# Batch 0's distances as float32r parts, the last product in two sets of columns, and a new order of loads

## The chip, the cores and the metric

The kernel runs on one core of one Trainium2 chip. A core has five engines that run their own instruction streams: TensorE (PE in the profile; its weight loads are PEld), VectorE (DVE), ScalarE (ACT), GpSimd (POOL) and SyncE (SP), which here issues all DMAs. The metric is the device time of one execution in microseconds (us). Before the change it is 393.94 us, the median of three runs (393.58 to 394.14).

## The reference

The inputs are x (4 batches, 256 tokens, 512 features), a context `ctx` (4, 64, 512), a table `fside` (4, 256, 256), a mask and weights, all float32. Four layers follow each other:

- L0, a mixture of low-rank updates: router weights `w = softmax(x @ router_W.T + b)`, `a_sum[b,s,r] = sum over a of x[b,s] . ctx[a,r]`, and `x = nan_to_num(x + 0.5 * sum_n w_n * (a_sum @ lora_B[n].T))`.
- L1, cross attention of 256 tokens on 64 context rows with 32 heads, an output product, a residual sum and a layer norm.
- L2 and L3, the same function twice, each with four blocks. Its core is:

```python
sq = jnp.sum(xyz * xyz, axis=1)                     # xyz = ctx: 64 coordinates, 512 points
d2 = sq[:, :, None] + sq[:, None, :] - 2.0 * jnp.einsum('bdn,bdm->bnm', xyz, xyz)
_, idx = jax.lax.top_k(-d2, 8)                      # 8 nearest points, once per batch
# in each block i:
c  = jnp.einsum('oi,bin->bon', w_center[i], p)      # p = leaky_relu(points)
gn = jnp.einsum('oi,bikn->bokn', w_neighbor[i], g)  # g = p gathered at idx
points = (c + gn.sum(axis=2)) / 9.0 + shortcut
```

`w_center` and `w_neighbor` are both `fside`, so a block is one product of `p` with `fside[i]` and one product with a 512 x 512 matrix of zeros and ones, "own point plus eight nearest".

## The kernel before

**A planner writes the order.** The functions of the kernel do not issue instructions. They add operations to a `Plan` (lines 63 to 167): engine, assumed cost, the tiles it reads and writes. `emit` then simulates all engines with those costs and always emits the operation that can start first; among operations of one engine that can start within 0.05 us the lowest `rank` wins. The rank is a due time: the entry of `DEADLINES` for the operation's batch (line 33) less the longest tail of work behind it. PSUM banks (8), SBUF buffers by kind, and the DVE/POOL shared port are resources of the simulation. The result is a fixed order per engine; on the chip each engine runs its order strictly, with semaphore waits. So any edit to an operation, a cost, a due time or the list of loads can move instructions everywhere.

**Loads.** `load` (line 258) adds DMAs on SP, in the order of the calls in lines 287 to 311, later ones through `load_xT` and `load_x` in the loop over batches. There are eight DMA semaphores, used in turn, so the ninth load waits for the first.

**Start.** PE runs 20 products of 128 columns on a constant (line 320) while the first loads travel. `keys` (line 677) makes K transposed from `WkT` and `ctxT` in four groups `kT`; `mixture` (line 386) makes the router logits and the low-rank input `route`; DVE turns them into `z`; `mix` (line 490) transposes `z` on PE (`zT`), multiplies by `lora_BT` (`upd`, line 505), adds to `x` (line 520), handles NaN and infinities (`hi`, `lo`, `odd`, copy_predicated in line 530) and transposes to `x1T`. `values` (line 731) makes V (`v`, then `vbd` on DVE, line 755), `queries` (line 764) Q (`q`, line 775), `attention` (line 798) the rest of L1.

**Distances.** `nearest` (line 614) takes four banks `d2_b_j` of 128 x 512, each holding x.x' - |x'|^2 / 2 for 128 points against all 512. For each bank DVE finds the eight largest (`top`, line 622) and replaces them (`rest`, line 625), ACT makes zeros and ones (`near`), POOL adds the identity, an SP DMA transposes, ACT stores `nbr`. For batches 1 to 3 `scores` (line 579) splits x into a float32r part and its exact rest, stacked on 128 partitions as `chl` and `clh`, and uses three float32r products a bank (lines 603 to 605); the rests are made on POOL. For batch 0 `scores_first` (line 544) uses float32 products with K = 64, two banks side by side in the upper and lower half of the array, which is why `ctx[0]` is loaded twice, into both halves of `cxx0`; only the squares are split (line 574).

**Blocks.** `block` (line 955) is done 8 times for each batch: ACT makes `p` (line 961), PE `wp` in float32 (line 972), ACT and DVE split it into `wph` and `wpl` (lines 985 and 988), PE multiplies both with `nbr` in float32r (line 1003, four products for each half of the points and each half `o` of the output), and DVE adds to `x` (line 1015). After the last block a DMA stores each 128 x 512 half (line 1025).

## Time and profile before

| | |
|---|---|
| median of 3 runs | 393.94 us |
| the profiled execution's own time | 394.15 us |
| its span, first to last instruction | 392.1 us |
| PE busy | 381.6 us (97%), 2116 products |
| PEld busy | 292.4 us (75%) |
| DVE busy | 226.8 us (58%) |
| ACT busy | 217.0 us (55%) |
| POOL busy | 105.3 us (27%) |
| mean granted TensorE clock | 0.996 |

Products are pipelined, so "busy" counts a product from its start to its modelled end and two neighbours overlap; the distance between two starts, the pitch, tells what a product costs in a stream. The chain of waits is followed back from the last instruction. A window gives the busy time of each engine between two times, the granted TensorE clock (1.00 is full speed) and what the DMAs moved.

### The profile page before, as it was taken

How to read it: one execution, taken by the hardware profiler on the slowest of the kernel's cores; microseconds unless marked ns; L12 is line 12 of the kernel's file. 1: busy time of each engine (PE TensorE's matmuls, PEld its weight loads, DVE VectorE, ACT ScalarE, POOL GpSimd, SP SyncE). 2: the span in 40 equal slices, each digit the busy share in tenths (PEclk: the TensorE clock that was granted, in tenths of full speed). 3: DMA queues.
4: the chain of work that ended last, by engine and by line, in shares of the span. 5: the costliest groups of instructions: out<-in, count | busy, mean ns of one | idle time of the engine just before them, and what ended most of it. 6: DMA issues, size and time to landing. Idle time of an engine off the chain costs nothing.

```text
span 392.1 us, 5547 instructions
## 1 busy us (share of the span) xinstructions
PE 381.6 (97%) x2116; PEld 292.4 (75%) x2116; DVE 226.8 (58%) x412; ACT 217.0 (55%) x335; POOL 105.3 (27%) x116
## 2 busy tenths in 40 slices
PE   8998999999999999999999999999999999999996
PEld 5847846657776866878767766888888888888884
DVE  2479799997796656945982524632433334324333
ACT  2651763966795989995697962333333422333330
POOL 4896204848205605640034220500000000000000
PEclk9998999999999999999999999999999999999999
DMA  6999320152401552434005411000000001000002
GB/s 185 369 381 354 69 54 0 28 109 44 91 15 24 115 80 54 63 72 82 1 2 99 90 28 55 0 0 2 0 0 2 0 0 55 0 1 2 0 0 107
DMA packets 47241, 25.80 MB, mean 66 GB/s; under 512 B 43184, under 2 KB 43312, under 8 KB 46576
## 3 DMA queue, kind: packets, MB, share of 16 engines
q1 hardware_dynamic: 47216, 25.46, 26.2%
q8 instruction: 16, 0.26, 0.3%
q14 instruction: 9, 0.07, 0.1%
HBM read 12.87 MB, written 2.10 MB: 38 GB/s over the span
## 4 chain that ended last, share of the span: by engine, by line
PE 71%; DVE 15%; ACT 8%; DMA 3%; issue 2%; SPq 1%; DVEq 0%; ACTq 0%
PE blk L1003 29%; PE wp L972 25%; PE q L775 4%; PE o L922 4%; PE upd L505 3%; PE kT L683 2%; DVE rest L625 2%; DMA WkT<-in_WkT 1%; DVE den L857 1%; PE avT L902 1%; DVE mx L842 1%; DVE s L848 1%; DVE top L622 1%; DMA pT_t<-pT_a 1%; ACT pTs L482 1%
## 5 line engine op out<-in xcount | busy, mean ns | idle before, releaser
L972 PE MATMUL wp<-fT,p 128*128 128x256 f32 x512 | 119.7, 380 | 1.4 <-ACT p L961 1.4
L1003 PE MATMUL blk<-nbr,wph 128*128 128x512 f32 x256 | 112.4, 439 | 0.3 <-ACT wph L985 0.3
L972 PEld LDWEIGHTS wp<-fT,p 128*128 128x128 f32 x512 | 96.3, 189 | 18.6 <-ACT p L961 2.4
L1003 PE MATMUL blk<-nbr,wpl 128*128 128x512 f32 x256 | 100.6, 393 | 0.7 <-DVE wpl L988 0.7
L1015 DVE SCALAR_TENSOR_TENSOR x<-blk,x 128x512 f32<-128x512 f32 x64 | 43.6, 686 | 72.3 <-PE blk L1003 72.2
L985 ACT CAST wph<-wp 128x512 fp32r<-128x512 f32 x64 | 37.2, 586 | 79.1 <-PE wp L972 79.0
L988 DVE TENSOR_TENSOR wpl<-wp,wph 128x512 fp32r<-128x512 f32 x64 | 43.7, 686 | 47.5 <-ACT wph L985 47.5
L961 ACT ACTIVATE p<-x 128x512 f32<-128x512 f32 x64 | 39.9, 629 | 35.2 <-DVE x L1015 34.1
L1003 PEld LDWEIGHTS blk<-nbr,wph 128*128 128x128 f32 x256 | 48.2, 188 | 13.0 <-issue 1.8
L1003 PEld LDWEIGHTS blk<-nbr,wpl 128*128 128x128 f32 x256 | 48.2, 188 | 12.7 <-DVE wpl L988 1.8
L879 POOL TENSOR_TENSOR s<-s,rden 128x512 f32<-128x512 f32 x32 | 32.3, 1043 | 70.5 <-DVE rden L869 41.4
L922 PE MATMUL o<-WoT,avTs 128*128 128x512 f32 x64 | 30.0, 598 | 0.3 <-ACT avTs L916 0.2
L775 PE MATMUL q<-x1T,WqT 128*128 128x256 f32 x128 | 29.2, 380 | 0.7 <-ACT x1T L457 0.7
L505 PE MATMUL upd<-lora_BT,zTs 128*128 128x512 f32 x64 | 28.7, 596 | 0.0
L482 ACT COPY pTs<-pT_t 128x1024 uint16<-128x1024 uint16 x24 | 27.1, 1160 | 1.4 <-DMA pT_t<-pT_a 1.2
L775 PEld LDWEIGHTS q<-x1T,WqT 128*128 128x128 f32 x128 | 24.2, 190 | 4.4 <-ACT x1T L457 1.0
L463 ACT COPY pT_a<-s 128x1024 uint16<-128x1024 uint16 x24 | 24.5, 1043 | 1.0 <-DMA pT_t<-pT_a 0.8
L854 ACT ACTIVATE s<-s 128x512 f32<-128x512 f32 x32 | 18.8, 625 | 9.1 <-DVE s L848 9.1
L842 DVE TENSOR_REDUCE mx<-s 128x8 f32<-128x512 f32 x32 | 20.1, 678 | 4.1 <-PE s L816 4.1
L505 PEld LDWEIGHTS upd<-lora_BT,zTs 128*128 128x128 f32 x64 | 11.9, 190 | 13.1 <-issue 12.2
L857 DVE TENSOR_REDUCE den<-s 128x8 f32<-128x512 f32 x32 | 20.1, 674 | 1.8 <-ACT s L854 1.7
L947 POOL TENSOR_TENSOR x<-x,rows 128x512 f32<-128x512 f32 x8 | 10.4, 1305 | 37.1 <-DVE x L942 37.1
(112 smaller groups left out, 402.2 us busy)
## 6 DMA issues: line engine op xcount, KB each, us to landing
xT<-in_xT SPq DMA_DIRECT2D x4, 512.0 KB, 7.5
x<-in_x SPq DMA_DIRECT2D x4, 512.0 KB, 11.8
out<-x SPq DMA_DIRECT2D x8, 256.0 KB, 2.0
WkT<-in_WkT SPq DMA_DIRECT2D x4, 256.0 KB, 7.4
lora_BT<-in_lora_BT SPq DMA_DIRECT2D x1, 1024.0 KB, 9.2
WvT<-in_WvT SPq DMA_DIRECT2D x1, 1024.0 KB, 10.4
rows<-in_rows SPq DMA_DIRECT2D x2, 512.0 KB, 10.8
WqT<-in_WqT SPq DMA_DIRECT2D x1, 1024.0 KB, 10.4
```

Source lines behind the costliest of these rows:

```text
L463: lambda: A_.copy(apart.tile.bitcast(U16).rearrange("p (t n) -> p t n", t=2), src().bitcast(U16).rearrange("p (n t) -> p t n", t=2),),
L482: lambda: A_.copy(dst().bitcast(U16).rearrange("p c (n t) -> p c n t", t=2), turned.tile.bitcast(U16).rearrange("p (t c n) -> p c n t", t= ...
L505: T_.matmul(ps2.tile, lhsT=zT.tile[:, bass.ts(c, 128)], rhs=w["lora_BT"][:, c, :], start=(c == 0), stop=(c == NC - 1),)
L775: T_.matmul(ps.tile[:, 0:S], lhsT=w["WqT"][:, c, bass.ts(o, 128)], rhs=x1T[b].tile[:, c, :], start=(c == 0), stop=(c == NC - 1),)
L879: lambda s=s, g=g: G_.tensor_tensor(heads(s), heads(s), rden.tile[:, bass.ts(g, HPC)].unsqueeze(2).to_broadcast([128, HPC, V]), ALU.mult,),
L922: T_.matmul(po.tile, lhsT=avT.tile[:, bass.ts(c, 128)], rhs=w["WoT"][:, c, :], start=(c == 0), stop=(c == NC - 1),)
L961: lambda l=l: A_.activation(p.tile[:, l], pt[:, l], AF.Prelu, alpha=SLOPE),
L972: T_.matmul(ps.tile[:, bass.ts(k, S)], lhsT=p.tile[:, c, bass.ts(2 * m2 + k, 128)], rhs=wi[:, c, :], start=(c == 0), stop=(c == NL - 1),)
L985: act(0.59, lambda ps=ps, hi=hi: A_.copy(hi.tile, ps.tile), (ps,), (hi,))
L988: lambda ps=ps, hi=hi, lo=lo: V_.tensor_tensor(lo.tile, ps.tile, hi.tile.bitcast(F32), ALU.subtract),
L1003: T_.matmul(pb[o].tile, lhsT=part.tile[:, bass.ds(m % 2 * S + o * 128, 128)], rhs=nbr[b, m], start=(m == 0 and k == 0), stop=(m == H // 12 ...
L1015: lambda o=o: V_.scalar_tensor_tensor(pt[:, o], pb[o].tile, 1.0 / (KNN + 1.0), pt[:, o], ALU.mult, ALU.add),
```

## The change

It does five things. (1) `scores_first`, `cxx0` and `csq0` go; batch 0 uses `scores` too, so `ctx[0]` is loaded once, and its three rests are made on DVE where the other batches use POOL. (2) The buffers of batch 2's `nbr` take `chl0` and `clh0` in place of `csq0` and `cxx0`. (3) The very last product group (batch 3, block 7, second half of points, `o = 1`) is done in `last`: two sets of 256 columns, four products each, then a sum and a store for each set. (4) The loads are reordered: `ctxT` comes second; batch 2's points come before `x(0)`; `rows1` and `x(2)` before batch 3's points and `x(1)`; the mask after those. (5) Due times of batches 1 and 2 and two assumed costs change.

```diff
-DEADLINES = (0.0, 32.0, 57.0, 64.0)
+DEADLINES = (0.0, 35.0, 60.0, 64.0)
...
-    csq0 = keep.tile([128, H], F32R, name="csq0")
-    cxx0 = keep.tile([128, H], F32, name="cxx0")
-    chl = {b: keep.tile([128, H], F32R, name=f"chl{b}") for b in range(1, B)}
-    clh = {b: keep.tile([128, H], F32R, name=f"clh{b}") for b in range(1, B)}
+    chl = {b: keep.tile([128, H], F32R, name=f"chl{b}") for b in range(B)}
+    clh = {b: keep.tile([128, H], F32R, name=f"clh{b}") for b in range(B)}
...
     load_points(0)
-    load("cxx2", 0.13, lambda: cxx0[64:128], a["ctx"][0])
+    load("ctxT", 0.5, lambda: ctxT.rearrange("p c b v -> p (c b v)"), a["ctxT"])
     load("small", 0.05, lambda: consts, a["small"])
-    load("ctxT", 0.5, lambda: ctxT.rearrange("p c b v -> p (c b v)"), a["ctxT"])
     load_k(0)
...
     load_w("WvT")
+    load_points(2)
     load_x(0)
-    load_points(2)
+    load("rows1", 0.5, lambda: rows1, a["rows1"].partition_broadcast(128))
+    load_x(2)
     load_points(3)
-    load("rows1", 0.5, lambda: rows1, a["rows1"].partition_broadcast(128))
+    load_x(1)
     load("mask_i", 0.12, lambda: mask_i.rearrange("p b v -> p (b v)"), a["mask"].partition_broadcast(128))
-    load_x(2)
-    load_x(1)
...
-    def scores_first(b, dist):
...
         def rest(out_, whole, upper, ins, key):
-            pool(
-                1.15,
-                lambda: G_.tensor_tensor(out_(), whole.tile[0:64], upper().bitcast(F32), ALU.subtract),
+            (pool if b else dve)(
+                1.22 if b else 0.69,
+                lambda: (G_ if b else V_).tensor_tensor(out_(), whole.tile[0:64], upper().bitcast(F32), ALU.subtract),
                 (whole, *ins),
                 (key,),
             )
...
-        (scores if b else scores_first)(b, dist)
+        scores(b, dist)
...
+                if (b, i, m2, o) == (B - 1, 2 * NBLK - 1, 1, NL - 1):
+                    continue
+                pe(0.94, gather, (*parts[m2], ("nbr", b, 2 * m2), ("nbr", b, 2 * m2 + 1)), (pb[o],))
+        if (b, i) == (B - 1, 2 * NBLK - 1):
+            last(b, pb, parts[1], pt)
...
+    def last(b, pb, parts, pt):
+        o = NL - 1
+        for h in range(2):
+            cols = bass.ts(h, H // 2)
+            pe(
+                0.52,
+                lambda cols=cols, h=h: [
+                    T_.matmul(
+                        pb[o].tile[:, cols],
+                        lhsT=part.tile[:, bass.ds(m * S + o * 128, 128)],
+                        rhs=nbr[b, 2 + m][:, cols],
+                        start=False,
+                        stop=(h == 1 and m == 1 and k == 1),
+                    )
+                    for m in range(2)
+                    for k, part in enumerate(parts)
+                ],
+                (*parts, ("nbr", b, 2), ("nbr", b, 3), *pb),
+                (("last", h),),
+            )
+        for h in range(2):
+            cols = bass.ts(h, H // 2)
+            dve(
+                0.38,
+                lambda cols=cols: V_.scalar_tensor_tensor(
+                    pt[:, o, cols], pb[o].tile[:, cols], 1.0 / (KNN + 1.0), pt[:, o, cols], ALU.mult, ALU.add
+                ),
+                (pb[o], ("x", b, o), ("last", h)),
+                (("out", h),),
+            )
+            plan.add(
+                "SP",
+                0.45,
+                lambda cols=cols: S_.dma_start(out=out[b, bass.ts(o, 128), cols], in_=pt[:, o, cols]),
+                (("out", h),),
+            )
```

The fixed order that comes out is new in many places. Those that the prediction uses: on PE, all products of batch 0's distances now stand behind the keys, the first bank (`d2_0_0`) between `zT` and `upd`, the other three between `v` of batch 0 and the two `route` groups of batches 1 and 2, with `v` of batch 1 after those; before, its four cross products and the first two products with the squares stood ahead of the keys, and two products with the squares behind `zT`. On DVE, the sums of `x(0)` are followed by `hi`, `lo`, `odd`, the mask's three operations, `vbd` of batch 0, three `top`, one `rest`, and only then by the copy_predicated that `x1T` waits for. The fourth distance bank of batch 3, with its `top`, `rest`, `near`, transpose and all four `nbr` stores, moves far back, behind the attention of batch 2.

## The prediction

> **What bounds the kernel now.** I read the page's busy times and slices first, then the chain of waits, then PE in order of time with the granted clock in windows of 1 us, PE's list of waits, and the last microseconds. The page:
>
> ```profile
> PE 381.6 (97%) x2116; PEld 292.4 (75%) x2116; DVE 226.8 (58%) x412; ACT 217.0 (55%) x335; POOL 105.3 (27%) x116
> PE   8998999999999999999999999999999999999996
> DVE  2479799997796656945982524632433334324333
> PEclk9998999999999999999999999999999999999999
> ```
>
> PE is busy from the third microsecond to the last, and for the second half of the span DVE has a third of it. So the end is PE's work, plus what PE idles or runs slowly, and that happens in slices 1 to 4. Slice 4 alone has a clock of 8 tenths. The chain over the first 37 us says who sets the time there:
>
> ```profile
> 3.13 5.58 DMA WkT<-in_WkT
> 8.84 1.97 PE kT L683 x8
> ...
> 19.11 5.21 PE upd L505 x12
> 24.34 0.69 DVE x L520
> 25.03 0.81 DVE mbias L719
> ...
> 34.09 0.74 DVE x L530
> 34.87 1.89 PE x1T L453 x8
> ```
>
> A load sets the first `kT`, then PE works without a break to `upd`, then DVE's row of work on `x(0)` up to copy_predicated (L530) sets `x1T`. What PE does in that time, in order (start, length, instruction; the bracket is idle time):
>
> ```profile
> 1.10 2.31 PE L320 MATMUL idle<-ones 128*128 128x128 bf16 x20 [1.10 <-DVE ones L314]
> 3.35 4.49 PE L561 MATMUL d<-cxx 64*128 64x512 f32 x8
> 7.76 0.73 PE L574 MATMUL d<-csq,mhalf_r 128*128 128x512 f32 x2
> 8.84 1.97 PE L683 MATMUL kT<-ctxT,WkT 128*128 128x256 f32 x8 [0.34 <-DMA WkT<-in_WkT]
> 29.55 3.79 PE L407 MATMUL route<-rw,xT 128*128 128x72 f32 x32
> ```
>
> The cross products of batch 0 (L561) and two with its squares (L574) fill the wait for `WkT`: they cost the end nothing, and they keep PE at work until 0.3 us before `kT`. The first row shows how PE starts: 20 products of 128 columns at a pitch of (2.31 - 0.31) / 19 = 0.105 us, where the float32r products of 512 columns further on take 0.233 us, 0.058 for 128. So PE seems to start at half speed, though the clock's row has 1.00 there. `kT`, with a pitch of (1.97 - 0.38) / 7 = 0.227 us a record, runs as fast as the same form does later (`wp`, 1.73 / 8 = 0.216). What idling does later stands in the clock (third figure from the right) of windows of 1 us:
>
> ```profile
> 33.00:34.00 1.00, 0.34 (x4) 1.00 1.01 418
> 34.00:35.00 1.00, 0.13 (x1) 1.00 1.02 422
> 35.00:36.00 1.00, 1.00 (x6) 0.50 0.96 397
> 38.00:39.00 1.00, 1.00 (x5) 0.79 0.61 98
> ```
>
> After `route` PE idles 1.53 us (33.34 to 34.87) and then runs at 0.50 until about 38.45: half of 3.45 us, 1.7 us, is lost.
>
> **The change, part by part.** The sum is made against the profiled execution, 394.15 us (span 392.1 and 2.05 around it), which is 0.21 above the median.
>
> *Loads.* One DMA of `ctx` less stands ahead of `WkT`: SP issues it 0.63 us earlier (1.41 less 0.78, the pitch of the two), and 128 KB less travels ahead, at most 0.55 us at the 240 GB/s of the window from 4 to 9 us. So `kT` starts between 0.3 and 1.2 us earlier, since later loads share the bandwidth; I take 0.9, at 7.9. -0.9 us.
>
> *The cover is gone.* PE has nothing between 3.4 and 7.9: 4.5 us of idling, three times the gap that halved the clock above, after a start that was at half speed anyhow. I take the same 3.45 us at half speed from 7.9 on, a loss of 1.7 us; bounds 0 (the clock holds) and 3.4 (twice as long). +1.7 us. `kT` to `upd` follow on PE without a break, so all of it is on the path; `z` (DVE, 12.58 to 16.64, on which `zT` waits) follows `route` by 4.1 us and then still ends before the keys.
>
> *Batch 0's distances on the path.* Twelve float32r products at 0.235 us (the chain has 0.23, 0.24 and 0.24 for those of batch 1 at 46.75), 2.8 us. Before, only two with the squares were on the path (the chain's 0.46 us at 18.65). +2.4 us; none of it hides, as PE stands in them behind `zT` and `v`, when everything it needs has long been made. The rests on DVE (3 x 0.69 by L551, where one was) and two casts more on ACT (0.6 each) lie between 3 and 7 us, where both engines idled.
>
> *DVE up to copy_predicated.* `upd` now ends at 27.0 (25.95 - 0.9 + 1.7 + 0.25 for the third product of the first bank). The second sum into `x(0)` waits for it. From there the order costs, by the rows of before: sum, `hi`, `lo`, `odd` with their waits for the port that POOL holds 4.4 (27.45 to 32.34, less 0.46 for the mask's reciprocal and product); the mask's three 1.4, which used to pass while DVE waited for `upd`; `vbd` of batch 0 0.86; the mask's last two 0.46; three `top` 1.8; three small ones of `route` 0.6; one `rest` 0.75; copy_predicated 0.74. That is 11.0 us, and `x1T` starts at about 38.2. PE's filler, 1.85 (`v`), 2.1 (three banks), 3.6 (`route`), 1.85 (`v`), lasts to 36.4. The gap is 1.8 us where it was 1.5, so the clock halves again as before: +0.3 us for the gap, nothing for the clock. Bounds: -1.7 (no second half-speed stretch) and +1.5 (POOL, with two more rests for batch 3 in this time, holds the port as it did in the 0.98 us of L428).
>
> The Trainium skill weighs this differently. Its page "TensorE: Matmul & The Clock Gate", Part 1, holds that PE falls to half speed after an idle window of about 3.4 us and recovers after as long a busy one. The first gap, 4.5 us, would halve the clock by that rule as by the row. The second, 1.8 us, would not by the rule, and then the sum would be 1.7 us lower; but the row has 0.50 after a gap of 1.53 us, so I go by the row.
>
> So PE is 0.9 less, 1.7 + 2.4 + 0.3 more: 3.5 us late at `x1T`.
>
> *New waits behind that.* The third and fourth `q` take banks that two `rest` free; DVE has these some 4 us after copy_predicated, PE comes to the banks at about 45.8, so 3 us of slack hide it. The mask lands about 1.1 MB (3 us) later than its 23.9, at 27, used at 32. SP's transposes of batch 0 still stand behind all loads, and their `nbr` is first used at 102.
>
> *What is given back.* PE idles later too:
>
> ```profile
> PE x1T L453 <- DVE x L530: 1.5, 1, 1.5
> PE wp L972 <- ACT p L961: 1.4, 2, 0.9
> PE q L775 <- ACT x1T L457: 0.7, 1, 0.7
> ```
>
> Besides the first, PE misses 0.82, 0.85 and 0.78 us in the three windows of 10 us from 80 to 110 and 1.23 us between 130 and 190, by its busy time: 3.7 us. DVE, ACT and POOL carry the work on which those wait. They are late by PE's delay, too, as `q` stands behind `x1T`. But the last distance bank of batch 3, one `top` and one `rest` (1.27 us of DVE) and `near` and four `nbr` (0.62 and 4 x 0.6 of ACT) move out of the crowded stretch. PE comes 3.5 us later, DVE about 2; I give back half of the 2.45 us before 110. Bounds 0 and 3.7. -1.2 us.
>
> *The end.*
>
> ```profile
> 388.04 1.27 SPq L1025 DMA_DIRECT2D out<-x  x2
> 388.26 0.69 DVE L1015 SCALAR_TENSOR_TENSOR x<-blk,x 128x512 f32<-128x512 f32 x1 [0.25 <-PE blk L1003]
> ```
>
> In the built program the first of the two new sums waits for the count of the very last product, and the second waits for no product at all: the two sums do not overlap the products, though the code has them in sets. Eight products of 256 columns cost 8 x 0.117 (half of 0.233) at best, the same 0.93 us as four of 512, and 8 x 0.216 (the pitch of `wp`'s records of 256) at worst, +0.8. Two sums of 256 columns at 0.43 (L755's 256 columns) are 0.86 where one was 0.69. The first store's issue (0.33) lies beside the second sum. A store of 256 KB takes 2.0 us to land and the 24 KB of `consts` took 2.2, so a half is no quicker. +0.2 us; bounds -0.35 (half of one sum hidden after all) and +1.1.
>
> The sum: -0.9 + 1.7 + 2.4 + 0.3 - 1.2 + 0.2 = +2.5, 396.65 against 394.15, and 396.4 against the median.
>
> **The rivals.** (a) *The delay is absorbed.* PE's idling after 80 us goes wholly, because PE is now later than the work that fed it: 394.15 + 3.7 - 3.7 = 394.15, which is no change against its own run. For it speak the relief of ACT, which has 19.65 of 20 us busy between 150 and 170; against it, that DVE and ACT start late themselves. It decides if PE's idling from 80 to 190 us falls below 1 us. (b) *The clock holds at the first `kT`*, the burst of 20 products being enough: 1.7 less, 394.7 against the median. Against it, the pitch of that burst. (c) *The clock holds at `x1T`*, the gap being filled by three more banks of work: also 1.7 less, and with (b) or (a) it is faster, 393.0 or less. For it: the filler grows by 2.1 us. (d) *The crowded stretch turns worse.* Three `top` and `rest` fall where DVE has 10.00 of 10 us busy (50 to 80 us): if their 3.9 us are all paid by DVE and then by PE, and nothing is given back, it is 396.4 + 1.2 + 2 = 399.6. Against it: DVE idled 2.5 us at 45 us, waiting for distances of batch 1.
>
> **How the numbers follow.** About 0.2% (0.8 us) is what a measurement can tell from no change. My forecast has 0.58, between 395 and 398.2; (a) 0.13, (b) alone 0.09, (c) alone or with another 0.10, (d) 0.10. Faster by over 0.8 us, below 393.15, needs (c) with (a) or (b), or all of (a) and a bit of luck: 0.11. Within it, 393.15 to 394.73: (a), (b) and some of (c): 0.14. Slower: 0.75. The range leaves out the far ends of (c) and (d): 393.2 to 399.4.
>
> **What would show it.** In the profile after: PE idle from 3.4 to near 7.9, then the records of `kT` at a pitch near 0.43 instead of 0.22; twelve products of batch 0 between `zT` and `route`; `x1T` of batch 0 at about 38 with a window of clock 0.50 behind it; less idling of PE between 80 and 110; both last sums behind the last product. I would be wrong if `kT` runs at full speed at once, or if PE loses its 3.7 us of later waits, or gains new ones: the order is new almost everywhere from 100 to 250 us, and I have priced that only by these bounds.

## The result and the profile after

The changed kernel takes 399.17 us, the median of four runs (398.36 to 400.8), beside 394.04 us for the kernel before on the same chip: a ratio of 1.0136, 95% interval 1.0115 to 1.0156. It is 5.1 us slower where +2.5 us was forecast. A second set of six runs on another occasion gave 399.74 us (1.0166, 1.0140 to 1.0192). The profiled execution of the changed kernel took 398.4 us with a span of 396.7 us, 4.6 us longer than the span before; it lies at the low end of its runs. The ratios leave out single runs more than 1.5% above the fastest of their kernel (one of e3_x1T1 below is such a run), while the medians in the tables count all runs.

The page of the changed kernel, busy times and slices:

```profile
PE 379.8 (96%) x2120; PEld 292.3 (74%) x2120; DVE 225.6 (57%) x415; ACT 218.3 (55%) x337; POOL 105.7 (27%) x116
PE   4997999989899999999999999999999999999996
DVE  2259989998598427894991744243432433334323
PEclk9999999999999999999999999999999999999999
```

PE's first slice is at 4 tenths where it was at 8, and slices 4, 9 and 11 (30 to 40, 79 to 89 and 99 to 109 us) are each one tenth lower than before. PE is busy for 1.8 us less although the end comes 4.6 us later: the loss is idling, all of it before 190 us. No slice has a lowered clock any more. The chain of waits over the first 39 us:

```profile
2.49 5.00 DMA WkT<-in_WkT
...
7.63 3.50 PE kT L641 x8
...
19.67 6.88 PE upd L497 x16
...
28.50 1.43 DVE lo L519
29.93 1.75 DVE odd L521 x2
31.68 1.27 DVE mbias L677
...
34.81 1.30 DVE top L580 x2
...
36.59 0.60 DVE top L580
37.19 0.67 DVE rest L583
37.86 0.65 DVE x L522
...
38.55 0.67 PE x1T L445 x4
```

The chain still goes from a load over PE to `upd` and then along DVE to copy_predicated (L522). But three `top` and a `rest` are new in DVE's part of it, and `mbias`, which stood ahead of the second sum into `x(0)`, now stands behind `odd`. PE's list of waits, the longest:

```profile
PE kT L641 <- DMA WkT<-in_WkT: 4.2, 1, 4.2
PE x1T L445 <- DVE x L522: 2.5, 1, 2.5
PE x1T L445 <- issue: 1.8, 1, 1.8
...
PE wp L930 <- ACT p L919: 0.9, 1, 0.9
```

The third line is new: PE's transposes of batch 1's `x` stand ahead of `v` of batch 2 and start at 83.60, 0.1 us after copy_predicated of `x(1)` ends (82.79 and 0.71 long on DVE); the view names no releaser ("issue"), so that this is the wait is read from these times.

Where the lateness arises is best read from the starts of the same groups in PE's timeline. "q to end" is the span less the start of `q`. The first two rows are the two kernels, the third the second profile of the changed one; the others belong to runs told below.

| profile | first kT | upd | x1T of batch 0 | q of batch 0 | wp of batch 0 | span | q to end |
|---|---|---|---|---|---|---|---|
| before | 8.84 | 18.95 | 34.87 | 38.81 | 95.43 | 392.1 | 353.3 |
| after | 7.63 | 19.51 | 38.55 | 41.12 | 98.71 | 396.7 | 355.6 |
| after, again (a_again) | 7.90 | 19.94 | 38.99 | 42.75 | 99.31 | 397.0 | 354.3 |
| b_cold | 8.74 | 21.10 | 36.57 | 39.94 | 96.68 | 393.7 | 353.8 |
| b_pe | 8.72 | 18.83 | 35.37 | 37.64 | 94.27 | 391.0 | 353.4 |
| b_dve | 8.78 | 18.89 | 39.07 | 43.13 | 99.76 | 396.6 | 353.5 |
| e1_warm | 8.46 | 18.80 | 38.08 | 41.71 | 98.44 | 396.6 | 354.9 |

So `x1T` is 3.7 to 4.1 us late, near the forecast (3.5). In these two profiles most of what differs from the forecast lies behind it. There the prediction had named a sign, less idling of PE between 80 and 110 us. The windows of the kernel before, then after (the second figure is PE's busy time):

```profile
80.00:110.00 30.00, 27.54 (x191) 1.00 0.41 78
```

```profile
80.00:110.00 30.00, 26.39 (x183) 1.00 0.34 71
```

The idling rose, from 2.46 to 3.61 us (3.41 in a_again).

### The profile page after: what moved, and what is told of

Same layout as the page of the kernel before. It is cut to its first block, busy times and chain, and to the rows that moved or that the text cites. A ratio compares the mean times of both kernels' runs of the same rounds, so it can differ in the third digit from the quotient of the medians.

```text
span 396.7 us, 5559 instructions
## 1 busy us (share of the span) xinstructions
PE 379.8 (96%) x2120; PEld 292.3 (74%) x2120; DVE 225.6 (57%) x415; ACT 218.3 (55%) x337; POOL 105.7 (27%) x116
## 4 chain that ended last, share of the span: by engine, by line
PE 64%; DVE 18%; ACT 9%; DMA 5%; issue 2%; POOL 1%; SPq 0%; DVEq 0%; ACTq 0%
PE blk L961 25%; PE wp L930 23%; PE o L880 4%; DMA pT_t<-pT_a 3%; PE q L733 3%; DVE den L815 2%; PE kT L641 2%; DVE s L806 2%; PE upd L497 2%; DVE mx L800 2%; DVE rest L583 1%; DVE top L580 1%; DVE lo L519 1%; DMA WkT<-in_WkT 1%; ACT pTs L474 1%
## 5 line engine op out<-in xcount | busy, mean ns | idle before, releaser
L961 PE MATMUL blk<-nbr,wph 128*128 128x512 f32 x254 | 110.1, 433 | 0.7 <-ACT wph L943 0.7
L880 PE MATMUL o<-WoT,avTs 128*128 128x512 f32 x64 | 28.9, 597 | 0.5 <-ACT avTs L874 0.5
L880 PEld LDWEIGHTS o<-WoT,avTs 128*128 128x128 f32 x64 | 11.8, 190 | 13.4 <-issue 12.3
```

What stands on the lines that cost most here:

```text
L880: T_.matmul(po.tile, lhsT=avT.tile[:, bass.ts(c, 128)], rhs=w["WoT"][:, c, :], start=(c == 0), stop=(c == NC - 1),)
L961: T_.matmul(pb[o].tile, lhsT=part.tile[:, bass.ds(m % 2 * S + o * 128, 128)], rhs=nbr[b, m], start=(m == 0 and k == 0), stop=(m == H // 12 ...
```

## First experiments: edits to the changed kernel

In the runs that move instructions, the planner first makes its whole list, the list is edited, and then the instructions are written out; without an edit the program is the changed kernel's. `find(engine, tile)` gives the operations of an engine that write a tile, `move(ops, at)` puts them ahead of `at`. All ratios are to the kernel before, run on the same chip.

| run | median us | ratio, 95% interval |
|---|---|---|
| e1_warm | 397.44 | 1.0082, 1.0062 to 1.0102 |
| e2_cp | 398.55 | 1.0113, 1.0089 to 1.0136 |
| e3_x1T1 | 401.13 | 1.0142, 1.0111 to 1.0173 |
| e4_all | 401.83 | 1.0194, 1.0168 to 1.0219 |
| a_again | 399.74 | 1.0166, 1.0140 to 1.0192 |
| p_dist | 407.96 | 1.0350, 1.0332 to 1.0367 |
| e5_mask | 398.41 | 1.0117, 1.0100 to 1.0135 |
| e6_early | 401.85 | 1.0199, 1.0185 to 1.0213 |
| e8_cp0 | 397.77 | 1.0100, 1.0075 to 1.0124 |
| e9_cp1 | 398.92 | 1.0128, 1.0108 to 1.0147 |
| e10_best | 402.76 | 1.0207, 1.0184 to 1.0229 |
| a_fewer | 398.41 | 1.0129, 1.0101 to 1.0158 |

**e1_warm: the cold start.**

```diff
-WARM = 20
+WARM = 80
```

> 80 dummy products at the start instead of 20, so that PE works until near the first kT; nothing else is changed, and the order is the same. Theory (the half speed of the first kT is on the path): the eight records of the first kT take about 2.0 us instead of 3.5, upd ends 1.5 us earlier, the second sum into x(0) and copy_predicated on DVE come 1.5 us earlier with it, and the kernel takes 1.5 us less than the changed kernel, about 397.7. Rival (absorbed): DVE or the transposes by DMA set the time of x1T or of the waits behind it, whatever PE does before; then the time changes by less than 0.4 us. Second rival: the dummy products end too late and hold back kT: the first kT starts after 8 us, and of the 1.5 us less than 1 is left.

By the ratios 2.1 us faster than the changed kernel (1.0082 against 1.0136, intervals apart). In its timeline the first `kT` takes 1.97 us; it starts at 8.46, held back by the dummy products until then. The runs also lie closer together, 397.25 to 398.32, where the two sets of the unchanged kernel reach from 398.36 to 402.17. A likely reason can be seen in the profile of e5_mask below, which fell on a long cold start (PE's timeline):

```profile
7.99 3.75 PE L667 MATMUL kT<-ctxT,WkT 128*128 128x256 f32 x8 [4.58 <-DMA WkT<-in_WkT]
11.54 3.52 PE L425 MATMUL route<-rw,xT 128*128 128x72 f32 x16
14.86 6.55 PE L667 MATMUL kT<-ctxT,WkT 128*128 128x256 f32 x24
```

Here not only the first `kT` (3.75 us) but all of `route` (3.52 where it is 1.90 in e1_warm) and some of the next keys run at half speed. From the first `kT` to `zT` it is 13.25 us; in the profile of the kernel before 8.77, and in e1_warm's too. Over the ten profiles that have neither batch 0's cross products nor more dummy products ahead of the first `kT`, this stretch is 1.5 to 4.5 us longer than 8.77, 2.4 on average. The profile after has 1.5, at the low end.

**e2_cp: copy_predicated first.**

```diff
+        mb = self.find("DVE", "mbias")[0]
+        self.move([self.find("POOL", f"hi0_{o}")[0] for o in range(2)], mb)
+        self.move([self.find("DVE", ("x", 0, o))[1] for o in range(2)], mb)
```

> The two copy_predicated into x(0) stand ahead of the mask's work on DVE (mbias, seen, some), of vbd and of the three top, instead of behind them; all other orders stay. Theory (DVE's row of work up to copy_predicated makes the gap of 2.48 us at x1T): copy_predicated at about 31.6 instead of 37.8, x1T of batch 0 directly behind v at about 36.1, no gap, and 2.5 us less for q; the wait on zTs1_1 (ACT) and the one on x1T of batch 1 stay, so the kernel takes 2 to 2.5 us less, about 397. Rival (the next wait takes it): what ACT and DVE have to do for batch 1 does not come earlier, so that PE's wait behind zTs1_1 or for upd1 grows by as much, and less than 1 us of the 2.5 is left at o0 (77.2 in the changed kernel).

About the same as the changed kernel (1.0113 against 1.0136, the intervals overlap). The gap went and came back one step on. Two rows of its timeline:

```profile
31.67 3.49 DVE L548 COPY_PREDICATED x<-odd,hi 128x512 f32<-128x512 uint8 x2
40.38 0.47 PE L587 MATMUL d<-chl 128*128 128x512 f32 x1 [2.86 <-DVE st L448]
```

The two copy_predicated took 3.49 us, not 1.34, while POOL worked on batch 3's rests, and PE waited 2.86 us at the first bank of batch 1: until 40.4, when the `rest` of batch 0 that frees this bank was just through on DVE (the bracket names the small operation beside it). DVE had the same work to do before PE could go on, in whatever order.

**e3_x1T1: the transposes of x(1) later.**

```diff
+        at = self.find("PE", "x1T1_1")[0]
+        self.move([self.find("PE", "x1T1_0")[0], self.find("ACT", ("x1T", 1, 0))[0]], at)
+        self.move([self.find("POOL", ("x", 1, 0))[0], self.find("SP", "xT3")[0]], at)
```

> The transposes of the first row block of x(1) on PE stand behind v(2) and the second o(0) instead of ahead of them, and what reads them on ACT, POOL and SP moves with them; all other orders stay. Theory (PE stands 1.78 us for copy_predicated of x(1), with v(2) and o(0) ready behind it): the wait goes, a shorter one before q of batch 1 may stay (0.7 us as in the kernel before), and the kernel takes 1.0 to 1.8 us less than the changed kernel, about 397.7. Rival: route(3), q of batch 1 and wp are set by DVE, ACT and the load of xT(3), which now starts later; then the wait moves to route(3), q or wp, and the time changes by less than 0.5 us.

No gain (1.0142). The rival holds: the wait of 1.78 us is gone, and `route` of batch 3 waits longer instead.

```profile
92.90 2.32 PE L425 MATMUL route<-rw,xT 128*128 128x72 f32 x10 [3.79 <-DMA xT<-in_xT]
```

The load of `xT(3)` is ordered behind the copy of these transposes, so their early place, with its wait, paid for an early load.

**e4_all: the three together, and zTs1_1 sooner.**

```diff
+        zt = self.find("ACT", "zTs1_1")[0]
+        self.move([self.find("PE", "zT1_1")[0], zt], self.find("ACT", ("nbr", 0, 0))[0])
```

> The three edits together (80 dummy products; copy_predicated of x(0) first; the first transposes of x(1) later) and a fourth: zTs1_1 on ACT ahead of the four stores of nbr(0), behind which PE waited 0.5 us for it. Theory (the loss of 5.1 us is four separate things, each on PE's path): 1.5 + 2.5 + 1.1 to 1.8 + 0.5 = 5.6 to 6.3 us less than the changed kernel, about 393, with the 2.4 us of the ten products more still in it. Rival (one limit lies behind them all: DVE and ACT, which have to do the same work before batch 1's attention): the gains overlap and the kernel stays above 396.

Not faster but slower than the changed kernel: 1.0194, clear of its first set of runs, though the interval of the second set overlaps. It has both new waits (2.86 us at the first bank of batch 1, 3.49 at `route` of batch 3), and 0.50 in the clock for 6.8 us from the middle of the first and for 3.4 us behind the second. So the theory of four separate losses on PE's path fell.

**a_again and p_dist.** The changed kernel once more, and its distances alone with the old loads and due times:

```diff
-DEADLINES = (0.0, 35.0, 60.0, 64.0)
+DEADLINES = (0.0, 32.0, 57.0, 64.0)
     load_points(0)
+    load("small", 0.05, lambda: consts, a["small"])
     load("ctxT", 0.5, lambda: ctxT.rearrange("p c b v -> p (c b v)"), a["ctxT"])
-    load("small", 0.05, lambda: consts, a["small"])
     load_k(0)
...
     load_w("WvT")
+    load_x(0)
     load_points(2)
-    load_x(0)
+    load_points(3)
     load("rows1", 0.5, lambda: rows1, a["rows1"].partition_broadcast(128))
+    load("mask_i", 0.12, lambda: mask_i.rearrange("p b v -> p (b v)"), a["mask"].partition_broadcast(128))
     load_x(2)
-    load_points(3)
     load_x(1)
-    load("mask_i", 0.12, lambda: mask_i.rearrange("p b v -> p (b v)"), a["mask"].partition_broadcast(128))
...
```

(Behind that, p_dist also has the old end: one product of 512 columns and one store.)

> The changed kernel unchanged, beside the others on the same chip. Expected: 398.4 to 399.9. If PE's half speed behind the gap at x1T of batch 0 (2.48 us) is on the path, runs with a granted clock of 1.00 are 1.4 us faster than runs with 0.995; if something else sets the time there, they are equal within 0.5 us, as the runs of the kernel before were (392.1 and 392.2 us of span at 1.00, 392.1 and 392.3 at 0.994 and 0.993).

> Batch 0's distances as in the changed kernel, all else as before: the old order of the loads (less the second load of ctx), the old due times, and one product of 512 columns and one store at the end. Theory A (PE's added products and the lost cover are the cost, by the prediction +1.7 and +2.4): the time stays near the changed kernel's, 398 to 399.5. Theory B (DVE's row of work between upd and copy_predicated sets the time; the new loads bring the mask so late that its three operations, 2.0 us, fall into that row): the mask's work lies in DVE's wait for upd again, x1T comes 1.5 to 2 us earlier than in the changed kernel, and the time is 396.5 to 397.5.

For a_again the expectation on the clock failed: its two runs at a granted clock of 1.00 were the longest, 401.95 and 402.17, and the four at 0.993 to 0.996 took 398.67 to 399.83. So half speed behind `x1T` is not what makes a run of the changed kernel long. The profiles agree: `q` of a_again is 1.63 us behind that of after, but `wp` only 0.60 and the end 0.3.

For p_dist neither theory foresaw 408 us. `x1T` of batch 0 comes at 37.11, 1.4 us earlier than after, as theory B said, and the kernel is 8.2 us slower than a_again. The planner's order behind it is another one, with waits of 1.3 us at 100 us, 2.0 at 153 and the longest at 200:

```profile
200.34 5.89 PE L930 MATMUL wp<-fT,p 128*128 128x256 f32 x14 [4.54 <-DVE s L806]
```

So the distances with the old loads and due times cost 14 us, and the new ones give 8 of them back. As the longest waits lie from 100 us on, I put that down to the order that follows from them; no run tells the order and the loads apart.

**e5_mask, e8_cp0: DVE's row shorter.** e5_mask moves the mask's work into DVE's wait for `upd`; e8_cp0 does that, puts copy_predicated straight behind `odd`, and POOL's two rests of batch 3 later:

```diff
+        self.move(self.find("SP", "mask_i"), self.find("SP", "rows1")[0])
+        work = [self.find("DVE", "mbias")[0], self.find("DVE", "seen")[0], self.find("DVE", "some")[0]]
+        self.move(work, self.find("DVE", ("x", 0, 1))[0])
```

```diff
+        at = self.find("DVE", ("vbd", 0))[0]
+        self.move([self.find("POOL", "hi0_1")[0]] + [self.find("DVE", ("x", 0, o))[1] for o in range(2)], at)
+        self.move([self.find("POOL", ("chl", 3, 1))[0], self.find("POOL", ("clh", 3, 0))[0]], self.find("POOL", "near1_0")[0])
```

> The changed kernel with the mask loaded ahead of rows1, and its first three operations on DVE (mbias, seen and the sum) between the two sums into x(0), where DVE waits 1.0 us for upd; all other orders stay. Theory B (DVE's row of work sets the time): copy_predicated 1.0 to 2.0 us earlier, the gap of 2.48 us at x1T shrinks to 0.5 to 1.5, and the kernel takes 1 to 2 us less than the changed one, about 397.5. Rival: the next wait takes it, as the wait of the first bank of batch 1 for its rest did when copy_predicated alone was moved; less than 0.5 us is left at the end.

> The changed kernel with the mask's work moved as in the run before it (its load ahead of rows1, three operations into DVE's wait for upd), and both copy_predicated of x(0) straight behind odd; two rests of batch 3 on POOL, which held DVE's port while copy_predicated stood alone in front (3.49 us for two instead of 1.34), come behind near0_3. Theory: x1T of batch 0 directly behind v, the gap of 2.48 us gone and no other in its place, since the first rest that frees a bank for batch 1 now ends at about 36: 2 to 2.5 us less than the changed kernel, 397 to 397.5. Rival: as before, the gap only moves (to a bank, to zTs1_1 on ACT, or to the transposes by DMA): no more than with the mask alone, 398.4.

Faster than a_again by 1.3 and 2.0 us by the medians, as theory B says for both; against the first set of runs the intervals overlap. The gap at `x1T` is 1.07 us in e5_mask's profile, and in e8_cp0's it is gone, with 0.77 us at the bank behind it. Both profiles had the long cold start (4.5 us). By their ratios the two still stay 4.6 and 3.9 us above the kernel before: with the gap at `x1T` gone, most of the loss is still there.

**e6_early, e9_cp1, e10_best.** e6_early puts batch 0's products, `top` and `rest` back to the start; e9_cp1 puts copy_predicated of `x(1)` first; e10_best is e8_cp0, e9_cp1, the move of zTs1_1 and 66 dummy products.

```diff
-WARM = 20
+WARM = 56
...
+        self.move([self.find("PE", f"d2_0_{j}")[0] for j in range(4)], self.find("PE", "kT0")[0])
+        self.move([self.find("DVE", f"top0_{j}")[0] for j in range(4)], self.find("DVE", "lg0")[0])
+        at = self.find("DVE", ("x", 0, 0))[0]
+        self.move([op for ops in zip(rest, near, mine) for op in ops], at)
...
```

(`rest`, `near` and `mine` are batch 0's `rest` on DVE and its `near` on ACT and POOL; three keys and one `zT` take other banks.)

```diff
+        at = self.find("DVE", "top3_0")[0]
+        self.move([self.find("POOL", "hi1_0")[0], self.find("DVE", ("x", 1, 0))[1]], at)
```

> The changed kernel with batch 0's twelve products ahead of the keys, in the time in which PE waits for WkT, its four top on DVE ahead of the router's work and its four rest behind it, and 56 dummy products at the start; three keys and one zT take other banks for it. The first kT then starts near 9.0 instead of 7.6, but at full speed. Theory B (the loss comes from batch 0's top and rest having moved from the idle time at 8 to 24 us into DVE's row of work between upd and x1T, and from the products behind v): DVE's row is 2.5 us shorter, PE's 2.8; x1T of batch 0 at about 35.5 instead of 38.55, and the kernel takes 3 to 4.5 us less than the changed one, about 395. Theory A (PE alone): kT at full speed gives 1.5 and the twelve products in the wait 2.8 less 1.4, together about 2.9: 396. Rival: PE's time before x1T does not count, since the loads and the transposes by DMA set the start of batch 1's work: above 398.

> The changed kernel with the first copy_predicated into x(1) on DVE ahead of three top and one rest of batch 3 (2.65 us) that stand in front of it; all else stays. Theory (PE's new wait of 1.78 us at x1T of batch 1 is DVE's order, and nothing else is late there): the wait goes, xT(3) is loaded 2 us earlier, and the kernel takes 1 to 1.8 us less than the changed one. Rival: what stands behind on DVE (the sum of o(0), top and rest of batch 3) is late by as much, and the wait comes back at route(3), at wp of batch 0 or at the first blk: less than 0.5 us.

> All together: 66 dummy products at the start (PE warm until the first kT at about 7.7), the mask's work and both copy_predicated of x(0) as in the run above, zTs1_1 on ACT ahead of the stores of nbr(0), and copy_predicated of x(1) first. Theory (separate losses): 2.3 for the dummy products (median of 397.44 against 399.7), 0.8 for a kT not held back by them, 2 to 2.5, 0.5 and 1 to 1.8: 6.6 to 7.9 us less than the changed kernel, 392 to 393. Rival (DVE, ACT or the transposes by DMA set the pace between 40 and 110 us, and what PE is given ahead of that is taken back there): above 396.

e9_cp1 changed nothing that can be measured: the wait of 1.78 us is gone, and `wp` waits 2.13 us for the second `p` where it was 0.90. e6_early and e10_best are slower than the changed kernel, by 2.1 and 3.0 us in the medians, though their intervals just overlap that of a_again. In e10_best `wp` of batch 0 starts 1.2 us earlier than after, and the first `blk` 1.7 us later. In e6_early they are 0.7 and 2.2 us later. In both, ACT waits in between for two transposes by DMA, which were issued at the same place as ever; the issues in the view of DMA from 99 to 108 us, first after, then e6_early:

```profile
zT_t<-zT_a SPq DMA_TRANSPOSE x2, 3.6
```

```profile
zT_t<-zT_a SPq DMA_TRANSPOSE x2, 5.0
```

They landed later (5.1 in e10_best), and `wph` stands behind them on ACT. Why they took longer was not tried and stays open, as does e10_best's loss, most of which comes after 150 us.

## Second experiments: one cost at a time in the kernel before

As each move in the changed kernel met another wait, the next runs left the old order alone and put one of the change's early costs into the kernel before, or took one out.

| run | median us | ratio, 95% interval |
|---|---|---|
| p_tail | 394.48 | 1.0011, 0.9998 to 1.0024 |
| b_cold | 395.83 | 1.0053, 1.0032 to 1.0073 |
| b_pe | 393.31 | 0.9981, 0.9971 to 0.9992 |
| b_dve | 399.04 | 1.0127, 1.0111 to 1.0142 |
| b_keep | 393.33 | 0.9979, 0.9964 to 0.9995 |
| b_move | 394.83 | 1.0024, 1.0005 to 1.0043 |

**p_tail: the end alone.**

```diff
+        final = (b, i) == (B - 1, 2 * NBLK - 1)
+        halves = [slice(0, H // 2), slice(H // 2, H)] if final else [slice(0, H)]
...
+                    for cols in halves if (m2, o) == (1, NL - 1) else [slice(0, H)]:
...
```

> The kernel before with the end alone: the last products, the last sum and the last store in two sets of columns, and the order of everything else kept. By the prediction +0.2 us (the sums do not overlap the products, two sums of 256 columns take longer than one of 512): 394.2, within the measurement of no change. Rival: two stores land sooner or the first sum overlaps after all: up to 0.35 us faster.

+0.1%, 0.3 us by the medians: near the forecast (+0.2), and by the interval not to be told from no change. The changed kernel's end shows why (DVE, then SP's queue): both sums lie behind the last product, 0.76 us together where one took 0.69, and the second store is issued behind them.

```profile
392.81 0.76 DVE L1016 SCALAR_TENSOR_TENSOR x<-blk,x 128x256 f32<-128x256 f32 x2 [0.26 <-PE blk L999]
```

```profile
393.26 0.83 SPq L1025 DMA_DIRECT2D out<-x  x2
```

**b_cold: the cover gone, alone.**

```diff
             def cross(k=k):
-                for j in (2 * k, 2 * k + 1):
-                    r = slice(64 * (j % 2), 64 * (j % 2) + 64)
-                    T_.matmul(
...
+                pass
...
-                    lambda j=j: T_.matmul(dist[j].tile, lhsT=mhalf_r, rhs=csq0, start=False, stop=True),
+                    lambda j=j: T_.matmul(dist[j].tile, lhsT=mhalf_r, rhs=csq0, start=True, stop=True),
```

> The kernel before without the eight cross products of batch 0 (left out, so the distances of batch 0 are its squares alone), in whose time PE waited for WkT: PE idles from 3.4 us to the first product with the squares near 7.7. The order stays. By the prediction's step (cover gone) +1.7 us, bounds 0 and 3.4; after the run with 80 dummy products in the changed kernel (2.3 us faster) I expect +1.5 to +2.5: about 396, and runs spread over 2 us or more, since the half speed lasted 3.5 us in some profiles and 7 in others. Rival: DVE's row of work sets x1T whenever upd ends, so the start costs less than 1 us.

+1.9 us by the medians: `upd` 2.15 later, `x1T` 1.70, the span 1.6. Together with e1_warm this shows that the cold start is on the path.

**b_pe: PE's products, alone.**

```diff
                 lambda l=l: [
+                    T_.matmul(ps.tile, lhsT=mhalf_r, rhs=csq0, start=True, stop=True)
+                    for _ in range(10 if (b, l) == (1, 0) else 0)
+                ]
+                + [
                     T_.matmul(
```

> The kernel before with ten more products of 128x512 in front of batch 1's route (their sums are overwritten), the order kept: 2.33 us of PE alone. By the prediction's step (batch 0's distances on the path) +2.4: 396.4. Theory D (DVE's row of work sets x1T, and PE's products lie beside it): the products fill the gap of 1.53 us at x1T, which comes 0.8 us later, and the half speed behind the gap goes: 0 to +0.8, at most 394.9.

Ten products more made the kernel faster, by 0.2% (0.6 us). PE's timeline:

```profile
29.43 2.58 PE L407 MATMUL route<-csq,mhalf_r 128*128 128x512 f32 x10
35.37 1.04 PE L457 MATMUL x1T<-ident,x 128*128 128x128 f32 x8
37.64 7.07 PE L779 MATMUL q<-x1T,WqT 128*128 128x256 f32 x32
```

PE comes from `route` straight to `x1T`, 0.5 us later than before, at full speed, and `q` is 1.2 us earlier. Theory D (DVE's row sets `x1T`, PE's products lie beside it) holds. **a_fewer** is the counterpart in the changed kernel:

```diff
+                less = b == 0 and j > 0
+                if not less:
-                T_.matmul(dist[j].tile, lhsT=mine, rhs=chl[b], start=True, stop=False)
-                T_.matmul(dist[j].tile, lhsT=mine, rhs=clh[b], start=False, stop=False)
+                    T_.matmul(dist[j].tile, lhsT=mine, rhs=chl[b], start=True, stop=False)
+                    T_.matmul(dist[j].tile, lhsT=mine, rhs=clh[b], start=False, stop=False)
```

> The changed kernel with one product instead of three in each of the last three banks of batch 0 (the two cross products left out, so these distances are the squares alone): 6 x 0.233 = 1.4 us less for PE between v and route. Theory D: x1T waits for DVE all the same, the gap of 2.48 us grows to 3.9, and the time stays within 0.5 us of the changed kernel's. Theory A: 1.4 us less.

Its ratio, 1.0129, is the changed kernel's within the intervals. That alone says little about 1.4 us, as the two sets of the changed kernel differ by 1.2 us themselves. The profile says more: the gap at `x1T` grew from 2.48 to 3.60 us, so PE waits for most of what it no longer computes.

**b_dve: DVE's row, alone.**

```diff
-        dve(0.74, lambda: V_.copy_predicated(v, odd.tile, hi.tile), (odd, hi), (key,), port=True)
+        dve(
+            0.74,
+            lambda: [V_.max(out=spare, in_=csq0.bitcast(F32)) for _ in range(0 if b or l else 6)]
+            + [V_.copy_predicated(v, odd.tile, hi.tile)],
...
```

> The kernel before with six more MAX8 of 128x512 (0.6 us each, 3.7 together) on DVE in front of copy_predicated of x(0), the order kept: it makes x1T as late as it is in the changed kernel (38.55 instead of 34.87), with no product more on PE. Theory D (DVE's row of work is what the end feels): +3 to +3.7, about 397.5. Theory A (PE's own time is what counts): the gap at x1T grows by 3.7, so it gives the same here, but then DVE and PE would add up in the changed kernel. Rival: batch 1's work has slack, and less than 2 us arrive at the end.

+5.1 us, as much as the changed kernel loses, with no product added and all else in its old place. (That the two sizes agree is in part chance: `x1T` is 0.5 us later here than in after, and the cold start is not in it.) From its timeline:

```profile
34.05 4.34 DVE L533 MAX8 spare<-csq 128x8 f32<-128x512 f32 x6
...
39.07 1.97 PE L454 MATMUL x1T<-ident,x 128*128 128x128 f32 x8 [5.79 <-DVE x L534]
```

The six took 4.34 us where 3.7 was expected (a pitch of 0.73, while two `top` stand 0.61 apart), `x1T` is 4.2 us late, `q` 4.3, `wp` 4.3, the span 4.5. Nothing is given back on the way. PE's idling between 80 and 110 us is what it was in the kernel before, 2.47 us where 2.46 was, though PE comes 4.3 us later:

```profile
80.00:110.00 30.00, 27.53 (x185) 1.00 0.40 67
```

The last column of the table says the same of all runs in the old order: from `q` to the end it is 353.1 to 353.8 us (b_keep and b_move 353.1 and 353.3), however late `q` is.

**b_keep and b_move: the gap of 1.53 us filled, in the kernel before.**

```diff
                 lambda: [
+                    T_.matmul(ps.tile[:, 0:128], lhsT=ones, rhs=ones, start=True, stop=True)
+                    for _ in range(24 if name == "x1T0_0" else 0)
+                ]
+                + [T_.transpose(ps.tile[:, bass.ts(c, 128)], src()[:, bass.ts(c, 128)], ident) for c in range(NC)],
```

```diff
+        self.move([self.find("PE", f"d2_1_{j}")[0] for j in range(2)], self.find("PE", "x1T0_0")[0])
```

> The kernel before with 24 dummy products of 128 columns (0.053 us each at full speed, 1.3 us) in front of the first transposes of x(0), into a bank that they overwrite; they wait for nothing that DVE still does there, so PE works through most of the gap of 1.53 us. The order is kept. Theory (the half speed behind the gap is on the path): no window of 0.50 behind x1T, q 1.2 to 1.5 us earlier than in the profile of before, and the kernel 0.6 to 1.4 us faster, 392.5 to 393.3, as with the ten products. Rival: the clock is as often lost as not in the kernel before, too (its runs have mean clocks from 0.993 to 1.00 and differ by 0.5 us), so that no more than 0.3 us is gained.

> The kernel before with the first two banks of distances of batch 1 (six products, 1.4 us) ahead of the transposes of x(0) on PE instead of behind them; all else is kept. They fill the gap of 1.53 us with work that is needed. Theory: no half speed, and 1.4 us less between x1T and q; as the two copies on ACT (0.6 us each) then lie between x1T and q with nothing beside them, some 0.6 us of that come back: q at about 36.6 instead of 38.8, and the kernel 1.3 to 2.2 us faster, 391.8 to 392.7. Rival: batch 1's chain on DVE and ACT (its rest, near and the stores behind them) sets the start of the scores, and the gain is no larger than with the dummy products.

b_keep is faster than the kernel before by as little as b_pe: 0.2%, 0.6 us. b_move, with real work in the gap, was to be 1.3 to 2.2 us faster and is 0.9 us slower than before. What holds `q` there can be read by setting two profiles of the same old order beside each other; first the kernel before (with half speed behind the gap), then p_tail (at full speed), rows around `x1T`:

```profile
35.88 0.17 DVE L428 TENSOR_TENSOR lg<-lg,st 128x16 f32<-128x16 f32 x1
36.04 2.52 POOL L540 TENSOR_TENSOR x<-x,rows 128x512 f32<-128x512 f32 x2 [2.51 <-DVE lg L428]
36.09 0.22 ACT L429 ACTIVATE lg<-lg 128x16 f32<-128x16 f32 x1 [9.28 <-DVE lg L428]
36.21 1.17 ACT L457 COPY x1T<-x1T 128x512 f32<-128x512 f32 x2
```

```profile
35.68 2.52 POOL L540 TENSOR_TENSOR x<-x,rows 128x512 f32<-128x512 f32 x2 [2.12 <-DVE lg L421]
35.89 1.10 DVE L428 TENSOR_TENSOR lg<-lg,st 128x16 f32<-128x16 f32 x1
37.03 0.22 ACT L429 ACTIVATE lg<-lg 128x16 f32<-128x16 f32 x1 [10.26 <-DVE lg L428]
37.15 1.05 ACT L457 COPY x1T<-x1T 128x512 f32<-128x512 f32 x2
...
38.26 0.92 PE L775 MATMUL q<-x1T,WqT 128*128 128x256 f32 x3 [0.69 <-ACT x1T L457]
```

ACT copies `x1T` for `q` behind an exponential of batch 1's router (L429), which waits for a small DVE subtraction (L428). In p_tail, where the transposes are quick, POOL's sum into `x` starts 0.2 us ahead of that subtraction, which then takes 1.10 us instead of 0.17, and ACT's copies come 0.94 us later. So the half speed behind the gap, 1.7 us of PE's time, cost `q` only 38.81 - 38.26 = 0.55 us. In b_pe POOL starts 0.27 us behind the subtraction, and no wait is left; in b_move, PE waits 2.07 us for those copies.

## Why the prediction was right and wrong

In short: PE was as late at `x1T` as forecast, and the step that failed is "what is given back". The prediction took 1.2 us off for PE's later idling; the runs gave nothing of it, and in three profiles 1.0 to 2.3 us more were lost from `q` to the end instead.

- **Direction and the lateness at x1T: right, with some luck.** 3.5 us late was forecast, 3.7 and 4.1 are measured. In the profile after, two misses nearly cancel: `upd` ended 0.5 us earlier than the 27.0 of the prediction, and DVE's row behind it took 12.1 us where 11.0 were counted (by the chain 5.1 instead of 4.4 from the sum to `odd`, 1.9 instead of 1.4 for the mask's three).
- **Loads (-0.9): right on the whole**, -1.2 in the profile. Over the ten profiles with the new loads in which `kT` waits for its load it starts between 7.23 and 9.40, 8.14 on average, where the seven with the old loads have 8.91; single profiles scatter by more than the term is worth.
- **The cover is gone (+1.7): the mechanism right, too small.** It cost 1.5 us in the profile and 2.4 on average over ten, up to 4.5; b_cold measured +1.9 and e1_warm 2.1 from the other side. This may be why most runs are slower than the profiled one; only profiles show the cold start, so it is not shown for the other runs.
- **Batch 0's distances on the path (+2.4): wrong, the step charged the wrong engine.** b_pe has -0.6 for as many products, a_fewer gains nothing clear by taking six away. DVE's row from the end of `upd` to the start of `x1T` grew by 12.1 - 8.9 = 3.2 us. The row had been priced (11.0 us), but its growth was booked as PE's products plus 0.3 for a longer gap. At `x1T` the sum is much the same either way, because that gap was worked out as the row's end less the end of PE's filler: fewer products would only have made the gap longer, as in a_fewer.
- **The clock at x1T ("halves again as before", nothing): not settled by one profile.** The same gap of 2.48 us was followed by full speed in the profile after and by 0.50 in a_again; windows of 1 us, third figure from the right, after and then a_again:

```profile
39.00:40.00 1.00, 0.94 (x8) 1.00 0.00 0
40.00:41.00 1.00, 1.00 (x6) 1.00 0.41 84
```

```profile
39.00:40.00 1.00, 1.00 (x5) 0.50 0.00 0
40.00:41.00 1.00, 1.00 (x6) 0.50 0.00 0
```

  Of the 1.63 us between the two at `q`, 0.44 were there at `x1T`; the other 1.2 go with the clock. Neither the row of before nor the rule decides it. The Trainium skill ("TensorE: Matmul & The Clock Gate", Part 1) also says that the window is free-running, so that the point of change varies; that fits these rows, while the gaps that lowered the clock here, from 1.53 us, are shorter than its 3.4 us.
- **What is given back (-1.2): wrong, and the step that failed.** In the old order nothing was given back: b_dve lost 4.2 us at `x1T` and 4.5 at the end, and idled as long between 80 and 110 us as the kernel before. In the new order the time from `q` to the end grew by 1.0 to 2.3 us (354.3 and 355.6 in the two profiles, 354.9 in e1_warm, against 353.3 before). Its visible pieces are the wait of 1.78 us for `x(1)`, where the kernel before waits 0.73 us ahead of `q` of batch 1, and in after 0.3 us behind zTs1_1 on ACT. The list of PE's idling before 110 us was read as slack that a late PE would use up; but in b_dve, with PE 4.3 us later, as much idling came back: the engines that cause it come late with `q`, too. a_again is the profile to hold against the sum, as its clock halved at `x1T` as assumed: 4.1 us late at `x1T`, 3.9 at `q`, 4.9 at the end, so that +1.0 stands where the sum has -1.2. In after the clock held, which gained 1.2 us at `q`, but from `q` to the end it lost 1.3 us more than a_again. Which part of the new order makes the extra 1.0 to 2.3 us stays open: e3_x1T1 and e9_cp1 each removed the wait for `x(1)`, and neither gained.
- **The end (+0.2): right as far as p_tail can tell** (+0.3, the interval includes nothing at all).

By the profile, 1.2 less for the loads, 1.5 for the cold start, 0.2 for the third product of the first bank and 3.2 for DVE's row make 3.7 at `x1T`; 1.4 less at `q`, where the clock held, and 2.3 more from `q` to the end: 4.6, as the spans differ. The medians differ by 0.5 to 1.1 more; a longer cold start in the other runs would do that, half speed at `x1T` would not (a_again's runs). That the changed kernel's loss is these costs and no more is not shown from its own side: e1_warm mends the cold start and e8_cp0 the gap at `x1T`, and they stay 3.2 and 3.9 us above the kernel before by their ratios; e10_best mends both and is slower.

Of the rivals, (c) happened in one profile, with 1.2 to 1.4 us at `q` that did not reach the end, and (d) named the right engine: three `top` and a `rest` of batch 0 stand in DVE's chain with 2.6 us, though before `x1T` and not in the stretch from 50 to 80 us.

## What to carry to other kernels

Before a product is charged to the path, ask what the next wait behind it waits for: here PE had 1.5 us to spare ahead of a chain on DVE, and a delay put into that chain (b_dve) cost its full length while ten more products on PE (b_pe) cost nothing. Idling that lies downstream of a delayed point is not slack for the delay unless the engine that causes it starts from something else; the cheapest test is to add the suspected cost, alone, to the kernel before. When a planner writes the order, price its reshuffling by a range of several microseconds: the same distances took 399.7 us with one order of loads and work and 408.0 with another, and most hand edits of the order moved a wait instead of removing it.

## What the runs showed of the hardware

- PE's half speed came in stretches of about 3.4 us or twice that (35.0 to 38.4 before, 42.1 to 45.5 in e2_cp, 38.2 to 45.0 in e4_all, 36.0 to 42.8 in b_dve). They start anywhere from inside the gap (b_dve: the gap lasts from 33.3 to 39.1) to 1.7 us behind it (e2_cp: it ended at 40.4), and gaps of the same length did or did not bring one: 1.53 us did in the profile of before, 1.57 did not in that of p_tail.
- At the very start the clock's row showed 1.00 while PE ran at half speed: the first `kT` took 3.50 us in the profile after, 1.97 with PE kept at work.
- Two copy_predicated of 128x512 took 3.49 us beside POOL's sums and 1.34 without them; a subtraction on 128x16 took 1.10 us where POOL had started 0.2 us before it, and 0.17 where POOL started later.
- Two transposes by DMA, issued at the same point of the program, landed after 3.6 us (median) in one kernel and 5.0 in another.
